# Cross-attention with layer norm on one core: another order of VectorE's work in the prologue

## The chip, the cores and the metric

The kernel runs on one core of one Trainium2 chip. The metric is the device time of one execution in microseconds (us). A core has TensorE (PE; its weight loads are shown apart as PEld), VectorE (DVE), ScalarE (ACT), GpSimd (POOL) and SyncE (SP), whose queue issues most of the DMAs. Each engine works through its own instructions in the order in which the program wrote them, and waits where an input or a buffer is not ready.

## The reference

For a batch of 4 with 2048 queries of width 512 and a context of 77 keys:

```python
qs = (q @ wq).reshape(Bq, Lq, H, HD).transpose(0, 2, 1, 3)
ks_ = (k @ wk).reshape(Bq, Lk, H, HD).transpose(0, 2, 1, 3)
vs = (v @ wv).reshape(Bq, Lk, H, HD).transpose(0, 2, 1, 3)
scores = jnp.einsum('bhqd,bhkd->bhqk', qs, ks_) / jnp.sqrt(jnp.float32(HD))
scores = jnp.where(mask[:, None, :, :], -jnp.inf, scores)
attn_w = jax.nn.softmax(scores, axis=-1)
attn = jnp.einsum('bhqk,bhkd->bhqd', attn_w, vs)
out = attn @ wo + q
mu = jnp.mean(out, axis=-1, keepdims=True)
var = jnp.mean((out - mu) ** 2, axis=-1, keepdims=True)
return (out - mu) / jnp.sqrt(var + EPS) * gamma + beta
```

There are 16 heads of width 32; `q` is x, and `k` and `v` are both the context. All is in float32.

## The kernel before, in words

The 8192 query rows make 64 tiles of 128 rows, 16 tiles to a batch. Two tiles are a pair, four are a group. Products of 512 columns are made in three parts from a high and a low part of each operand (wqh and wql, xth and xtl, and so on). The high part is a copy on ScalarE, the low part a subtraction on VectorE or GpSimd.

The order of the work is written out by hand: the program's order is each engine's order. PSUM is one ring of 8 banks (`bank`), taken in TensorE's order, so a product waits until what lay in its bank eight allocations earlier has been read out. Dependencies go by the region of a tile that an instruction touches.

The **prologue** (lines 558 to 622) loads and splits the inputs and makes the queries of the first group (pq, L591 and `q_visit`, L173) and all keys (pk, `keys_part`, L192), which ScalarE and VectorE copy to kct (`keys_evac`, L205).

The **loop** (lines 635 to 734) takes one pair per pass, u being its first tile. For a tile t the steps are:

- `scores(t)` (L289): 64 matmuls on TensorE into four banks.
- `maxima(t, lo, hi)` (L307): VectorE, 16 instructions (one per head) that add the mask's bias mb and find the row's maximum; they write pbuf, of which there are three.
- `exps(t)` (L324): ScalarE, 16 exponentials with their sums.
- `recip(t)` (L336) on VectorE and `normalise(t)` (L340) on GpSimd.
- `transp(t)` (L359): VectorE, blocks of 32x32 into B. B has two buffers, and the first two uses of them are ctx_f and ctx_h, the context in the prologue.
- `regroup(b)` (L381): twelve DMAs on SP for a pair, from B to PT.
- `av(b)` (L390): the attention product of a pair on TensorE, 32 matmuls from PT and vsb into two banks (pa). `av_hi` and `av_lo` split it for `o_proj` (L452), then come `residual`, `moments`, `scale`, `affine` and `store`, some passes later.

In the first passes other work lies between these steps. `mask_bias(b, ts)` (L277) makes mb from the mask for the tiles ts of a batch, two instructions on VectorE. `mask_nan(b)` (L282) is a row check that makes nz from the mask, three instructions. `split_wv` (L255) makes the low parts of wv on VectorE. `values(r)` (L231) makes the values of batch r on TensorE, 12 matmuls into one bank (pv), and `values_evac(r)` (L240) copies them to vsb with VectorE in two instructions: batch r, and those rows of the last batch that were dealt to the same product. `load_xT`, `cast_xT` and `split_xT` bring a group's x; a new `load_xT` on SP waits until `split_xT` on GpSimd has released its buffer. `split_wo` makes the low parts of wo on GpSimd. `q_visit` and `q_evac` make a quarter of a group's queries: passes 0, 2 and 4 have extra ones (`early`, L625).

From tile 54 on, a written list of steps (`ORDER`, L45) takes the place of the loop. The change does not touch it.

VectorE's order in the first passes is, in the program's order: mask of tile 0, keys, maxima of tile 0 with a q copy in the middle, mask of tiles 1 to 15, low parts of wv, q copy, reciprocal 0, maxima 1, transpose 0, row check, reciprocal 1; then maxima 2 with two q copies in the middle, transpose 1, value copy 0, two q copies, reciprocal 2, maxima 3, value copies 1 and 2, reciprocal 3; then maxima 4, transposes 2 and 3, two q copies, reciprocal 4, maxima 5.

Of the kernel before, what the change touches and what calls it, by code (L numbers as in the profile page):

```python
# [67 lines left out]
def xattn_layernorm(  # L68
# [17 lines left out]
    TPB = mask.shape[2]  # L86
# [57 lines left out]
    def keys_of(h):  # L144
        return slice(TAIL_K, NK2) if h % 2 == 0 else slice(0, NK)
# [3 lines left out]
    od, pos, mvs, rns, vd, ris, ends = {}, {}, {}, {}, {}, {}, {}  # L149


    def load_xT(g, c):
        fx[g, c] = sb.tile([P, 2, GRP], F32, tag="xtf", name=f"xtf_{g}_{c}")
        nc.sync.dma_start(fx[g, c], xT[g, :, c : c + 2])
# [29 lines left out]
    def q_evac(g, m):  # L184
        pq = qp.pop((g, m))
        if g:
            nc.vector.tensor_copy(qd[g][:, m, :], pq)
        else:
            nc.vector.tensor_copy(qd[0][:, m : m + 2, BLK:], pq.rearrange("p (m r) -> p m r", m=2))
# [15 lines left out]
    def keys_evac(pks, m):  # L205
        for i, eng in ((m, nc.scalar), (m + 1, nc.vector)):
            pk = pks[i][:, : NB * (NK + 1)].rearrange("p (b k) -> p b k", b=NB)[:, :, :NK]
            for dst, src in ((kct[:, i, :, TAIL_K:], pk), (kct[:, i, :, :TAIL_K], pk[:, :, NK - TAIL_K :])):
                if eng is nc.scalar:
                    eng.activation(dst, src, AF.Copy, scale=KSCALE)  # L210
                else:
                    eng.tensor_scalar(dst, src, KSCALE, None, ALU.mult)
# [18 lines left out]
    def values(r):  # L231
        pv = bank(f"pv_{r}")
        n = 0
        for c in range(NC_D):
            for i, v in ((0, wvh), (0, wvl), (1, wvh)):
                nc.tensor.matmul(pv, ctx_s[c][i][:, r, :], v[c], start=(n == 0), stop=(n == 11))
                n += 1
        vd[r] = pv

    def values_evac(r):  # L240
        pv = vd.pop(r)
        for b, p0, k0, n in ((r, 0, 0, NK2), (NB - 1, NK2, 32 * r, 32)):
            src, dst = (a.rearrange("p (q a d) -> p q a d", a=2, d=HD) for a in (pv[p0 : p0 + n], vsb[k0 : k0 + n, b]))
            rows_of = vm[k0 : k0 + n, :, 0][:, None, :, None].to_broadcast((n, NP, 2, HD))
            nc.vector.tensor_tensor(dst, src, rows_of, ALU.mult)
# [9 lines left out]
    def split_wv():  # L255
        for c in range(NC_D):
            nc.vector.tensor_tensor(wvl[c], stage_b[:, 0, c], wvh[c].bitcast(F32), ALU.subtract)
# [19 lines left out]
    def mask_bias(b, ts=slice(0, TPB)):  # L277
        mb, nz, m8 = bat[b]
        nc.vector.tensor_scalar(mb[:, ts, TAIL_K:], m8[:, ts], MASKED, None, ALU.mult)
        nc.vector.tensor_scalar(mb[:, ts, :TAIL_K], m8[:, ts, NK - TAIL_K :], MASKED, None, ALU.mult)  # L280

    def mask_nan(b):  # L282
        mb, nz, m8 = bat[b]
        nc.vector.tensor_reduce(nz, m8, AX.X, ALU.min)
        nc.vector.tensor_scalar(nz, nz, 3.0e38, 10.0, ALU.mult, ALU.mult)
        nc.vector.tensor_scalar(nz, nz, 0.0, EPS, ALU.mult, ALU.add)
# [20 lines left out]
    def maxima(t, lo, hi):  # L307
        pb = pbuf[t % NPB]
        mb = bat[t // TPB][0]
        nm = nmax[t]  # L310
        for h in HEADS[lo:hi]:
            g, j = divmod(h, GH)
            nc.vector.tensor_tensor_reduce(  # L313
                pb[:, h // 2, (h % 2) * NK : (h % 2 + 1) * NK],
                scs[t][j][:, g * NK : (g + 1) * NK],
                mb[:, t % TPB, keys_of(h)],
                -1.0,
                3.0e38,
                ALU.add,
                ALU.min,  # L320
                accum_out=nm[:, h : h + 1],
            )
# [13 lines left out]
    def recip(t):  # L336
        ris[t] = sb.tile([P, H], F32, tag="ri", bufs=3, name=f"ri_{t}")
        nc.vector.reciprocal(ris[t], sums[t])  # L338

    def normalise(t):  # L340
        pv = pbuf[t % NPB][:, :, : 2 * NK].rearrange("p q (a k) -> p q a k", a=2)
        rv = ris[t].rearrange("p (q a) -> p q a", a=2)[:, :, :, None]
        nc.gpsimd.tensor_tensor(pv, pv, rv.to_broadcast((P, NP, 2, NK)), ALU.mult)  # L343
# [15 lines left out]
    def transp(t):  # L359
        b, tt = divmod(t, 2)  # L360
        if b not in bts:
            bts[b] = sb.tile([P, 5, 2 * NP * 32], F32, tag="B", name=f"B_{b}")
        if b < NBLK - 1:
            bt = bts[b].rearrange("p c (q t r) -> p c q t r", q=NP, t=2)[:, :, :, tt, :]
        else:
            bt = bts[b].rearrange("p c (t q r) -> p c q t r", q=NP, t=2)[:, :, :, tt, :]
        nc.vector.transpose(  # L367
            bt.rearrange("p c q r -> p q c r"),
            pbuf[t % NPB].rearrange("p q (c r) -> p q c r", c=5),
        )  # L370
# [238 lines left out]
        split(*(a[:, c : c + 2, BLK:] for a in gx[0]), f0[c][:, 1])  # L609
    deal_last()  # L610
    q_visit(0, 0)
    mask_bias(0, slice(0, 1))
    gate(stage_a[:, 1, NC_D - 1, D - 1 :])
    load_wv()
    for m in range(0, NG, 2):
        keys_evac(pks, m)
    for c in range(0, NC_D, 2):
        fx[1, c] = stage_a[:, 0, c : c + 2]
        nc.sync.dma_start(fx[1, c], xT[1, :, c : c + 2])
# [8 lines left out]
    def visits(u):  # L628
        return early[u] if u in early else [divmod(u + 5, 4)] * (u + 5 < 4 * NGRP)

    def pieces(u):
        return casts.get(u) or [((u + 8) // 4, u % 4)] * (u + 8 < 4 * NGRP)

    evac = [(0, 0)]
    for u in range(0, 2 * CUT, 2):
        n = u // 2
        m, k = divmod(u, TPB)

        for q in pieces(u + 2):
            if u >= 4:  # L640
                load_xT(*q)
        for t in (u - 4, u - 3):
            if t >= 0:
                load_x(t)
        scores(u)
        maxima(u, 0, H // 2)
        for q in evac:
            q_evac(*q)
        maxima(u, H // 2, H)
        for q in pieces(u):  # L650
            cast_xT(*q)
        exps(u, 0, H)
        for q in pieces(u):
            split_xT(*q)
        if u == 0:
            mask_bias(0, slice(1, TPB))
            split_wv()
        if u >= 6:
            o_proj(u - 6)
        for v in {2: (0,)}.get(u, ()):  # L660
            values(v)
        for q in visits(u):
            q_visit(*q)
        if u >= 6:
            residual(u - 6)
            moments(u - 6)
        if u == 4:
            transp(2)
        if u == 2:
            load_xT(*pieces(4)[0])  # L670
        if u:
            transp(u - 1)
            regroup(n - 1)
        for v in list(vd):
            values_evac(v)
        if u >= 8:
            scale(u - 8)
            scale(u - 7)
        if u >= 8:
            affine(u - 8)  # L680
        for q in visits(u):
            q_evac(*q)
        if u == 0:
            load_wo()
            nc.gpsimd.memset(ident, 0.0)
            nc.gpsimd.affine_select(ident, ident, [[-1, P]], ALU.not_equal, 1.0, base=0, channel_multiplier=1)
        if k == TPB - 6 and m + 1 < NB:
            load_mask(m + 1)
        if k == TPB - 4 and m + 1 < NB:
            mask_bias(m + 1)  # L690
        if k == TPB - 2 and m + 1 < NB:
            mask_nan(m + 1)

        recip(u)
        if u >= 4:
            av(n - 2)
            av_hi(n - 2, 0)
            av_hi(n - 2, 1)
        scores(u + 1)
        maxima(u + 1, 0, H // 4)  # L700
        if u >= 4:
            av_lo(n - 2, 0)
        maxima(u + 1, H // 4, H // 2)
        if u >= 4:
            av_lo(n - 2, 1)
        maxima(u + 1, H // 2, H)
        normalise(u)
        for c in {0: (0, 1), 2: (2, 3)}.get(u, ()):
            split_wo(c)
        if u >= 8:  # L710
            affine(u - 7)
        exps(u + 1, 0, H // 4)
        exps(u + 1, H // 4, H)
        if u >= 5:
            o_proj(u - 5)
        if u >= 5:
            residual(u - 5)
        if u != 2:
            transp(u)
        for v in {2: (1, 2)}.get(u, ()):  # L720
            values(v)
            values_evac(v)
        evac = visits(u + 1)
        for q in evac:
            q_visit(*q)
        if u >= 5:
            moments(u - 5)
        if u == 0:
            mask_nan(0)
        recip(u + 1)  # L730
        normalise(u + 1)
        if u >= 8:
            store(u - 8)
            store(u - 7)
# [8 lines left out]
    visits = {"Q": q_visit, "q": q_evac}  # L743
# [81 lines left out]
```

## Time and profile before

| what | value |
|---|---|
| time, median of 3 runs | 518.78 us (516.29 to 519.95) |
| the profiled execution's own time | 517.11 us |
| its span in the profile | 515.3 us, mean granted clock 0.996 |
| DMA | 110.24 MB, 214 GB/s |
| TensorE at work from / first scores | 1.18 us / 21.65 us |
| first attention product | 54.58 us |
| last attention product in the loop's form | 474.24 us |

A row of the timeline has the start in us, the duration, engine, line and operation, what it writes and reads by the program's names, and a count where equal neighbours are merged; in brackets stand the idle time just before it and what seems to have ended it. In the page the busy times of each engine, their share of the span and the number of instructions come first, then 40 equal slices of the span with a digit for each (9 is 90% or more). The releaser of a wait is inferred from semaphores; where the named engine had long been done, it was another.

### The profile page before, as it was taken

How to read it: one execution, taken by the hardware profiler on the slowest of the kernel's cores; microseconds unless marked ns; L12 is line 12 of the kernel's file. 1: busy time of each engine (PE TensorE's matmuls, PEld its weight loads, DVE VectorE, ACT ScalarE, POOL GpSimd, SP SyncE). 2: the span in 40 equal slices, each digit the busy share in tenths (PEclk: the TensorE clock that was granted, in tenths of full speed). 3: DMA queues.
4: the chain of work that ended last, by engine and by line, in shares of the span. 5: the costliest groups of instructions: out<-in, count | busy, mean ns of one | idle time of the engine just before them, and what ended most of it. 6: DMA issues, size and time to landing. Idle time of an engine off the chain costs nothing.

```text
span 515.3 us, 20436 instructions
## 1 busy us (share of the span) xinstructions
PE 504.5 (98%) x6838; PEld 385.7 (75%) x6838; DVE 473.8 (92%) x2572; ACT 470.3 (91%) x2241; POOL 418.1 (81%) x375
## 2 busy tenths in 40 slices
PE   9999989999999999999999999999999999999994
PEld 6987767777777777777777777777777877777672
DVE  5699998899999888989999898889999989999996
ACT  6789999999899999999899999999899999999841
POOL 0658549889799988888889989889889988857996
PEclk9999999999999999999999999999999999999998
DMA  8946678787778878788778878869878887776665
GB/s 304 402 146 161 175 201 206 205 233 207 202 186 229 222 217 226 211 215 223 182 208 235 232 199 213 227 178 240 216 201 220 212 217 232 203 200 176 170 215 209
DMA packets 58936, 110.24 MB, mean 214 GB/s; under 512 B 9392, under 2 KB 11312, under 8 KB 58832
## 3 DMA queue, kind: packets, MB, share of 16 engines
q1 hardware_dynamic: 56144, 103.62, 72.6%
q0 software_dynamic: 2128, 4.85, 3.4%
q8 instruction: 55, 0.90, 0.8%
q10 hardware_dynamic: 560, 0.46, 0.3%
q14 instruction: 49, 0.40, 0.3%
HBM read 41.79 MB, written 16.78 MB: 114 GB/s over the span
## 4 chain that ended last, share of the span: by engine, by line
PE 74%; DVE 8%; POOL 5%; DMA 4%; SPq 3%; ACT 3%; issue 2%; DVEq 0%; POOLq 0%; ACTq 0%
PE po L463 30%; PE pq L170 26%; PE pa L397 9%; PE sc L299 9%; ACT pbuf L327 2%; SPq L379 2%; DVE B L367 2%; DMA PT<-B 2%; DVE pbuf L313 2%; DMA stage_b<-wo 1%; DMA stage_a<-wk 1%; POOL mvt L529 1%; POOL o_end L542 1%; DVE AL L432 1%; POOL o_end L493 1%
## 5 line engine op out<-in xcount | busy, mean ns | idle before, releaser
L327 ACT ACTIVATE pbuf<-pbuf,nm 128x77 f32<-128x77 f32 x1024 | 352.4, 349 | 17.3 <-DVE nm L313 15.8
L327 ACT ACTIVATION_READ_ACCUMULATOR pbuf<-pbuf,nm 128x1 f32 x1024 | 194.0, 189 | 0.0
L313 DVE CUSTOM_DVE_ANT_0 pbuf<-sc,mb 128x77 f32<-128x77 f32 x1024 | 170.5, 230 | 22.3 <-PE sc L299 22.2
L343 POOL TENSOR_TENSOR pbuf<-pbuf,ri 128x1232 f32<-128x1232 f32 x63 | 142.2, 2258 | 23.5 <-DVE ri L338 19.4
L170 PE MATMUL pq<-xth,wqh 128*128 128x512 f32 (+1 forms) x256 | 98.8, 386 | 0.0
L170 PE MATMUL pq<-xtl,wqh 128*128 128x512 f32 (+1 forms) x256 | 97.9, 382 | 0.0
L170 PE MATMUL pq<-xth,wql 128*128 128x512 f32 (+1 forms) x256 | 97.9, 382 | 0.0
L367 DVE STREAM_TRANSPOSE B<-pbuf 128x1280 f32<-128x1280 f32 x64 | 95.5, 1493 | 2.2 <-DMA PT<-B 1.7
L463 PE MATMUL po<-woh,AH 128*128 128x512 f32 x232 | 96.8, 417 | 0.0
L463 PE MATMUL po<-wol,AH 128*128 128x512 f32 x232 | 90.7, 391 | 0.0
L463 PE MATMUL po<-woh,AL 128*128 128x512 f32 x232 | 88.8, 391 | 0.0
L313 DVE DVE_READ_ACCUMULATOR2_ANT nm<- 128x1 f32 x1024 | 83.9, 82 | 0.0
L493 POOL TENSOR_TENSOR o<-o,gam 128x512 f32<-128x512 f32 x50 | 65.6, 1312 | 14.4 <-ACT o L489 14.3
L299 PEld LDWEIGHTS sc<-kct,q 32*64 32x64 f32 x4096 | 51.4, 130 | 24.2 <-issue 23.5
L494 POOL TENSOR_TENSOR o<-o,bet 128x512 f32<-128x512 f32 x50 | 64.5, 1289 | 3.9
L163 POOL TENSOR_TENSOR xtl<-xtf,xth 128x1024 fp32r<-128x1024 f32 x28 | 67.0, 2394 | 0.0
L299 PE MATMUL sc<-kct,q 32*64 32x77 f32 x4096 | 61.5, 237 | 0.3 <-DVE nm L313 0.3
L397 PE MATMUL pa<-PT,vsb 96*32 96x256 f32 x960 | 58.0, 382 | 1.9 <-DVE st L471 1.3
L170 PEld LDWEIGHTS pq<-xth,wqh 128*128 128x128 f32 x256 | 48.1, 188 | 9.8
L170 PEld LDWEIGHTS pq<-xth,wql 128*128 128x128 f32 x256 | 48.1, 188 | 9.4
L170 PEld LDWEIGHTS pq<-xtl,wqh 128*128 128x128 f32 x256 | 48.1, 188 | 9.1
L463 PEld LDWEIGHTS po<-woh,AH 128*128 128x128 f32 x232 | 43.5, 187 | 12.5 <-issue 0.7
(139 smaller groups left out, 700.5 us busy)
## 6 DMA issues: line engine op xcount, KB each, us to landing
PT<-B SPq DMA_DIRECT2D x352, 128.0 KB
xtf<-xT SPq DMA_DIRECT2D x28, 512.0 KB
o<-x SPq DMA_DIRECT2D x56, 256.0 KB
out<-o SPq DMA_DIRECT2D x56, 256.0 KB
PT<-B POOLq DMA_DIRECT2D x20, 128.0 KB, 4.0
o_end<-x SPq DMA_DIRECT2D x8, 256.0 KB
out<-o_end SPq DMA_DIRECT2D x8, 256.0 KB
xtf<-xT SPq DMA_DIRECT2D x4, 256.0 KB
```

The source lines that it names most:

```text
L163: nc.gpsimd.tensor_tensor(l, fx.pop((g, c)), h.bitcast(F32), ALU.subtract)
L170: nc.tensor.matmul(pq, w[:, c, m * P : (m + 1) * P], r[:, c, rs], start=(n == 0), stop=(n == 11))
L299: nc.tensor.matmul(sc[j][half : half + P // 2, g * NK : (g + 1) * NK], qs[q, g, r0 : r0 + P // 2], kct[q, g, t // TPB, keys_of(j)], start= ...
L313: nc.vector.tensor_tensor_reduce(pb[:, h // 2, (h % 2) * NK : (h % 2 + 1) * NK], scs[t][j][:, g * NK : (g + 1) * NK], mb[:, t % TPB, keys_ ...
L327: nc.scalar.activation(pb[:, h // 2, (h % 2) * NK : (h % 2 + 1) * NK], pb[:, h // 2, (h % 2) * NK : (h % 2 + 1) * NK], AF.Exp, bias=nmax[t ...
L343: nc.gpsimd.tensor_tensor(pv, pv, rv.to_broadcast((P, NP, 2, NK)), ALU.mult)
L367: nc.vector.transpose(bt.rearrange("p c q r -> p q c r"), pbuf[t % NPB].rearrange("p q (c r) -> p q c r", c=5),)
L379: queue.dma_start(pts[b][32 * c : 32 * c + 32, i, :, cols], src)
L397: nc.tensor.matmul(pas[b, g // 2][HD * j : HD * (j + 1), (g % 2) * BLK : (g % 2 + 1) * BLK], vsb[:, 2 * b // TPB, HD * h : HD * (h + 1)], ...
L463: nc.tensor.matmul(pos[t], a[:, c, rs], w[:, c, :], start=(first and n == 0), stop=(n == 11))
L493: nc.gpsimd.tensor_tensor(o, o, gam, ALU.mult)
L494: nc.gpsimd.tensor_tensor(o, o, bet, ALU.add)
```

## The change

Seven edits, all in VectorE's order of the first three passes, with the GpSimd and DMA steps that go along:

- The first piece of the mask covers tiles 0 to 7 (before: tile 0); the rest, tiles 8 to 15, stays in pass 0.
- The row check of batch 0 stands behind the key copies in the prologue (before: behind transpose 0).
- The low parts of wv and reciprocal 0 stand behind the second tile's maxima (before: ahead of them).
- Reciprocal 1 and normalise 1 stand between the halves of the third tile's maxima (before: at the end of pass 0).
- Transpose 0 moves to the second pass, then value copy 0, then transpose 1; the two q copies of that pass move behind the maxima of tile 3.
- Value copy 1 follows its product; transpose 2 stands at the end of the second pass, ahead of the maxima of tile 4 (before: behind them).
- Value copy 2 moves behind transpose 3 and the second regroup.

```diff
-    mask_bias(0, slice(0, 1))
+    mask_bias(0, slice(0, TPB // 2))
...
         keys_evac(pks, m)
+    mask_nan(0)
...
         maxima(u, 0, H // 2)
+        if u == 2:
+            recip(1)
+            normalise(1)
         for q in evac:
             q_evac(*q)
...
         if u == 0:
-            mask_bias(0, slice(1, TPB))
-            split_wv()
+            mask_bias(0, slice(TPB // 2, TPB))
...
-        if u == 4:
-            transp(2)
         if u == 2:
             load_xT(*pieces(4)[0])
+        if u == 2:
+            transp(0)
+            values_evac(0)
         if u:
             transp(u - 1)
             regroup(n - 1)
-        for v in list(vd):
-            values_evac(v)
+        if u == 4:
+            values_evac(2)
...
-        for q in visits(u):
-            q_evac(*q)
+        if u != 2:
+            for q in visits(u):
+                q_evac(*q)
...
-        recip(u)
+        if u:
+            recip(u)
...
         maxima(u + 1, H // 2, H)
+        if u == 0:
+            split_wv()
+            recip(0)
+        if u == 2:
+            for q in visits(u):
+                q_evac(*q)
         normalise(u)
...
-        if u != 2:
+        if u >= 4:
             transp(u)
-        for v in {2: (1, 2)}.get(u, ()):
-            values(v)
-            values_evac(v)
+        if u == 2:
+            values(1)
+            values_evac(1)
+            values(2)
...
-        if u == 0:
-            mask_nan(0)
-        recip(u + 1)
-        normalise(u + 1)
+        if u:
+            recip(u + 1)
+            normalise(u + 1)
+        if u == 2:
+            transp(2)
```

## The prediction

> **What bounds the kernel now.** I read the page first (busy shares and slices), then what TensorE waits for, then the timelines of all engines up to 100 us, and the chain of waits last. TensorE is busy for almost the whole span, and the granted clock is full in nearly every slice:
>
> ```profile
> PE 504.5 (98%) x6838; PEld 385.7 (75%) x6838; DVE 473.8 (92%) x2572; ACT 470.3 (91%) x2241; POOL 418.1 (81%) x375
> PEclk9999999999999999999999999999999999999998
> ```
>
> The ends of matmuls are modelled, so a busy share alone proves little. The next rows do more. First the busy times of each engine in stretches (PE, PEld, DVE, ACT, POOL, then clock, DMA share, GB/s), then TensorE's instructions in order of time, then its two waits of over 0.3 us in the whole run, of which the second is before its first instruction:
>
> ```profile
> 67.00:67.50 0.50, 0.00 (x0) 0.00 (x0) 0.47 (x2) 0.50 (x4) 0.50 (x1) 1.00 0.58 209
> 83.20:98.20 15.00, 15.00 (x211) 11.39 (x210) 13.43 (x79) 14.51 (x71) 13.21 (x12) 1.00 0.81 221
> ```
>
> ```profile
> 54.58 1.93 PE L397 MATMUL pa<-PT,vsb 96*32 96x256 f32 x32
> ...
> 66.30 0.39 PE L170 MATMUL pq<-xtl,wqh 128*128 128x512 f32 x1
> 66.53 0.39 PE L170 MATMUL pq<-xth,wql 128*128 128x512 f32 x1
> 68.22 0.42 PE L397 MATMUL pa<-PT,vsb 96*32 96x256 f32 x4 [1.30 <-DVE st L471]
> ...
> 83.20 1.93 PE L397 MATMUL pa<-PT,vsb 96*32 96x256 f32 x32
> ```
>
> ```profile
> PE pa L397 <- DVE st L471: 1.3, 1, 1.3
> PE pw L565 <- DVE ident L558: 1.2, 1, 1.2
> ```
>
> Equal matmuls start 0.23 us apart though each lasts 0.39 (66.30, 66.53): they follow at TensorE's own pace. From one attention product to the next (68.22, 83.20, end of the stretch at 98.20) a pair of tiles takes 15.0 us, all of it TensorE, while ScalarE has 14.51 of work in the stretch and VectorE 13.43. So in the steady loop TensorE sets the time. An earlier VectorE gains nothing there. In the prologue, too, TensorE runs without a wait from about 5 us to 66.92 (66.53 + 0.39). Then it stands still for 1.30 us, ahead of the second pair's attention product. **That one gap is all that a new order of VectorE's prologue can win.** The row names bn_stats (DVE st), but the product does not read it; it reads PT, which the SP queue's transfers write:
>
> ```profile
> 41.19 0.33 SPq L154 DMA_DIRECT2D xtf<-xT  x1
> 41.62 8.86 SPq L379 DMA_DIRECT2D PT<-B  x12
> ...
> 51.15 0.92 SPq L446 DMA_DIRECT2D o<-x  x2
> 56.17 9.22 SPq L379 DMA_DIRECT2D PT<-B  x12
> 65.48 0.53 SPq L154 DMA_DIRECT2D xtf<-xT  x1
> ```
>
> ```profile
> 49.88 2.69 DMA PT<-B
> ```
>
> The first regroup starts at 41.62 and by the chain of waits (second fence) lands at 52.57, 10.95 us later; its product runs at 54.58. The second starts at 56.17, as soon as the transposes below end at 56.13; the product starts at 68.22, 12.05 us later. I take 10.95 to 12.05 us from start of a regroup to data.
>
> **The change, part by part.** VectorE's rows that carry the sums:
>
> ```profile
> 16.79 0.19 DVE L279 TENSOR_SCALAR mb<-m 128x77 bf16<-128x77 uint8 x1
> ...
> 18.01 0.62 DVE L212 TENSOR_SCALAR kct<-pk 128x308 f32<-128x308 f32 x2 [0.95 <-PE pk L196]
> 18.89 0.62 DVE L212 TENSOR_SCALAR kct<-pk 128x308 f32<-128x308 f32 x2 [0.26 <-PE pk L196]
> 22.59 0.24 DVE L313 CUSTOM_DVE_ANT_0 pbuf<-sc,mb 128x77 f32<-128x77 f32 x1 [3.07 <-PE sc L299]
> ...
> 25.72 1.35 DVE L279 TENSOR_SCALAR mb<-m 128x1155 bf16<-128x1155 uint8 x1
> ...
> 27.21 1.28 DVE L257 TENSOR_TENSOR wvlAH<-stage_b,wvh 128x512 fp32r<-128x512 f32 x2
> ...
> 29.61 0.68 DVE L189 COPY q<-pq 128x512 f32<-128x512 f32 x1
> 30.21 0.24 DVE L338 RECIPROCAL ri<-sum 128x16 f32<-128x16 f32 x1
> 32.85 1.50 DVE L367 STREAM_TRANSPOSE B<-pbuf 128x1280 f32<-128x1280 f32 x1
> 34.28 1.39 DVE L284 TENSOR_REDUCE nz<-m 128x16 f32<-128x1232 uint8 x1
> ...
> 36.21 0.25 DVE L338 RECIPROCAL ri<-sum 128x16 f32<-128x16 f32 x1
> ...
> 42.87 1.29 DVE L187 COPY q<-pq 128x512 f32<-128x512 f32 x2
> ...
> 46.71 2.81 DVE L245 TENSOR_TENSOR vsb<-pv,small 96x512 f32<-96x512 f32 x4
> ...
> 53.23 2.90 DVE L367 STREAM_TRANSPOSE B<-pbuf 128x1280 f32<-128x1280 f32 x2 [0.19 <-issue]
> ```
>
> Unit costs from these starts: both mask instructions for 15 tiles 1.49 (25.72 to 27.21); the row check 1.93 (34.28 to 36.21); low parts of wv 2.40 (27.21 to 29.61); 16 maxima with a reciprocal 2.64 (30.21 to 32.85); a transpose 1.43; two q copies 1.25; one value evacuation (two of the four instructions) 1.4. Nothing is added or removed but the split of the mask (still two pairs of instructions); no DMA is added. The other engines:
>
> ```profile
> 30.59 0.36 ACT L327 ACTIVATE pbuf<-pbuf,nm 128x77 f32<-128x77 f32 x1 [2.11 <-DVE nm L313]
> 36.08 1.99 ACT L159 CAST xth<-xtf 128x1024 fp32r<-128x1024 f32 x2
> ```
>
> ```profile
> 30.54 2.26 POOL L343 TENSOR_TENSOR pbuf<-pbuf,ri 128x1232 f32<-128x1232 f32 x1 [4.41 <-DVE ri L338]
> 32.76 2.55 POOL L267 TENSOR_TENSOR wol<-stage_b,woh 128x512 fp32r<-128x512 f32 x2
> 36.54 2.26 POOL L343 TENSOR_TENSOR pbuf<-pbuf,ri 128x1232 f32<-128x1232 f32 x1 [1.24 <-DVE ri L338]
> 38.77 4.74 POOL L163 TENSOR_TENSOR xtl<-xtf,xth 128x1024 fp32r<-128x1024 f32 x2
> ```
>
> ```profile
> 32.16 0.95 PE L299 MATMUL sc<-kct,q 32*64 32x77 f32 x64
> 41.44 0.95 PE L299 MATMUL sc<-kct,q 32*64 32x77 f32 x64
> 48.01 0.95 PE L299 MATMUL sc<-kct,q 32*64 32x77 f32 x64
> ```
>
> *Mask and row check.* Eight tiles' mask from 16.79 cost about 0.8 (half of 1.49), at most all of it: done by 17.6, latest 18.3, against the key copies at 18.01, which wait for TensorE. A slip of 0.3 is covered: the first maxima stand idle for 3.07 us until 22.59. The row check from 19.5 (18.89 + 0.62) ends at 21.4, also ahead of 22.59. Price zero.
>
> *Second tile's maxima ahead of the low parts.* From 25.72: mask half 0.8, q copy 0.6, so the maxima run from 27.2 to 29.7 instead of 30.4 to 32.85. ScalarE is free at 28.5 (30.59 less its idle 2.11), and starts the second tile's exponentials 2.1 earlier; they take 5.5 (30.59 to 36.08): 28.5 to 34.0. The low parts run 29.7 to 32.1, the reciprocal to 32.3. Who waits for the low parts: TensorE's first value product, just behind the scores at 32.16, thus 33.1. Slack 1 us.
>
> *GpSimd and SP.* The first normalise starts at 32.3 instead of 30.54; two normalises, two wo parts and the first xT half keep GpSimd busy until 41.8 instead of 41.2. The xT load on SP (41.19) waits for that half, and the regroup stands behind it: 42.2 instead of 41.62. It lands at 53.2 (10.95 later) to 54.3, and TensorE wants it at 54.58. Hidden, with 0.3 to 1.4 to spare.
>
> *The next pair on VectorE.* Scores at 32.16 end at 33.1. First half of the maxima to 34.4, reciprocal 1, two q copies, second half: 37.1. Transpose 0 to 38.5, value evacuation 0 to 39.9, transpose 1 to 41.4 (normalise 1 ends 39.4). Exponentials of tile 2, behind ScalarE's casts, 36.0 to 41.5. Maxima of tile 3 when the scores at 41.44 end: 42.4 to 44.9 (before: from 44.2). The two q copies moved behind them end at 46.2, and TensorE wants them for the scores at 48.01: slack 1.8. Value evacuation 1 to 47.6. Exponentials of tile 3 end at 48.1, reciprocal 3 to 48.4. Transpose 2 overwrites the buffer of ctx_h, which the last value product reads until 48.0: 48.4 to 49.9. Maxima of tile 4 to 52.4, transpose 3 to 53.9, against 56.13 before.
>
> *What this is worth.* The second regroup starts at 53.9, 2.2 earlier; SP is free by 52.7 (its loads end at 52.07, plus 0.6). Data is there at 64.9 to 66.0; TensorE arrives at 66.92. The gap of 1.30 closes with about 1 us to spare.
>
> *What is late next.* Value evacuation 2 now stands behind transpose 3: 53.9 to 55.3. It frees the bank of the second half of the first attention product, which starts about 0.96 after 54.58, at 55.5. Cost 0, with only 0.2 to spare; from below it cannot gain, from above I allow 0.5. The third regroup (started at 69.70, so data 80.7 to 81.8) now meets TensorE at 81.9 instead of 83.20: 0 to 0.2 lost at worst.
>
> **Sum.** 1.30 less 0 (at worst 0.7) leaves 1.3 us. The profiled execution took 517.11 us (span 515.3 and 1.8 around it): 515.8. The median shown is 518.78 of 516.29 to 519.95, 1.67 above it; taking off the same 1.3 gives 517.5, the number I predict.
>
> The Trainium skill, "Perfetto Trace Analysis", section "Identifying the Most-Contended Engine", speaks against my bound: it says that matmul busy share is a poor measure of headroom and weight-load share a good one. By that the 75% of PEld would leave room in TensorE, and the time would be that of the third rival below. The 15.00 us loop without a gap speaks against it.
>
> **Rivals.**
> Given back or not closed in full: the third regroup, or the tail, which the chain of waits puts on GpSimd, keeps part of it. 0.3 to 1.0 us less: about 518.1.
> The wait at 66.92 is not the transfer's: then nothing changes, 518.8. For it: the row names VectorE. Against: the named instruction isn't read there.
> TensorE has hidden slack, and VectorE's whole lead of 2.2 to 2.3 counts: 516.5. Against: the 0.23 pace.
> Slower: value evacuation 2 behind transpose 3 holds TensorE inside the first attention product. It decides from an evacuation that ends 1.3 past 55.5, thus at 56.8, if VectorE runs 1.5 later than my replay. At 2.5 late, TensorE loses 2.3 there, the old gap is covered, net +1.0: 519.8.
>
> One more slower case needs a stall far longer: TensorE standing for some microseconds and then running on at a lower clock. The row at 67.00 shows the clock at 1.00 within the gap of 1.30, so a stop of that size costs only itself. The Trainium skill, "TensorE: Matmul & The Clock Gate", section "HAM oscillation — how this bites in real kernels", says that gaps above roughly 3.4 us throttle the clock; no run here shows one. With 3.4 lost and as much again at half pace it would be an estimated 5.1, less the 1.3: about 522.6.
>
> **How the numbers follow.** Gap closes: 0.62 (517.5). In part: 0.17 (518.1). No effect: 0.08 (518.8). Hidden slack: 0.04 (516.5). Slower at the evacuation: 0.07 (519.8). A stall not foreseen that costs over 1%: 0.02. About 1%, 5 us, is what a measurement of this kernel can tell from no change; only the last reaches it. The runs spread by 2.5 below and 1.2 above their median, so 517.5 gives 515.0 to 518.7; the partial, neutral and part of the slower case take the upper end to 519.5. Slower by over 1%: 0.04, with a share for what a replay cannot see; faster by over 1%: 0.02, since the gap is all there is to win; within: 0.94.
>
> **What would show it.** First maxima still at 22.59; tile 1's exponentials from 28.5; low parts behind the second tile's maxima with TensorE's value product still at 33.0; the second regroup on SP at about 54; the second attention product at 66.9 with no idle time, the third at 81.9. I am wrong if TensorE shows a wait between 22 and 66 us (look at 33, 48 and 55.5 first), if the 1.3 stays with an earlier regroup, or if it comes back at 81.9.

## The result and the profile after

The changed kernel takes 524.76 us in the median of 4 runs (523.88 to 526.04), the one before 518.68 (4 runs): 1.0134 of the time, 95% interval 1.0103 to 1.0165. It was forecast 1.3 us faster, at 517.5; it is 6.1 us slower, outside the range. The profiled execution, the slowest of the four, took 526.04 us (span 524.2).

What TensorE waited for, in total, by the profile of the changed kernel (us, times, longest):

```profile
PE sc L299 <- DVE vsb L245: 2.1, 1, 2.1
PE sc L299 <- DVE nm L313: 1.3, 4, 0.4
PE pa L397 <- DVE nm L313: 1.2, 1, 1.2
PE pw L565 <- DVE ident L558: 1.2, 1, 1.2
PE po L463 <- issue: 0.9, 1, 0.9
PE pa L397 <- PE pq L170: 0.6, 1, 0.6
```

The old wait ahead of the second attention product is gone. In its place stand waits at scores and ahead of and inside the first product. All but two are put down to VectorE: the 0.9 at a projection (issue), and the 0.65 ahead of the first product, which comes as the first regroup's data land. TensorE's rows in order of time show where (the second and third products end the list):

```profile
33.64 0.95 PE L299 MATMUL sc<-kct,q 32*64 32x77 f32 x64
...
56.78 1.07 PE L397 MATMUL pa<-PT,vsb 96*32 96x256 f32 x16 [0.65 <-PE pq L170]
59.06 1.07 PE L397 MATMUL pa<-PT,vsb 96*32 96x256 f32 x16 [1.21 <-DVE nm L313]
60.06 0.58 PE L299 MATMUL sc<-kct,q 32*64 32x77 f32 x4
60.96 0.48 PE L299 MATMUL sc<-kct,q 32*64 32x77 f32 x2 [0.32 <-DVE nm L313]
63.58 1.37 PE L299 MATMUL sc<-kct,q 32*64 32x77 f32 x58 [2.13 <-DVE vsb L245]
...
66.33 0.63 PE L170 MATMUL pq<-xth,wqh 128*128 128x512 f32 x1
66.75 0.63 PE L170 MATMUL pq<-xtl,wqh 128*128 128x512 f32 x1
...
75.68 1.93 PE L397 MATMUL pa<-PT,vsb 96*32 96x256 f32 x32
...
90.68 1.93 PE L397 MATMUL pa<-PT,vsb 96*32 96x256 f32 x32
```

Set against the rows of before, TensorE is 1.5 us late at the third scores (33.64 against 32.16), 2.2 at the first product (56.78 against 54.58) and 7.5 at the second (75.68 against 68.22), with the closed gap of about 1.3 already taken off. The third is at 90.68 against 83.20, again 7.5: the loss is all made by 69 us, and the loop then runs at the same 15 us a pair. The rest, up to the 8.9 between the two profiled executions (526.04 and 517.11), comes far later, with the 0.9 at a projection (issue) that this execution has and the one before has not.

The matmuls at 66.33 and 66.75 start 0.42 apart, where they stood 0.23 apart before. The clock (the column behind POOL's) says why:

```profile
59.00:60.20 1.20, 1.14 (x18) 0.64 (x18) 1.20 (x17) 1.20 (x8) 0.00 (x0) 1.00 0.02 7
60.20:61.50 1.30, 0.93 (x6) 0.52 (x5) 1.30 (x9) 1.30 (x9) 0.00 (x0) 0.74 0.00 0
61.50:63.50 2.00, 0.00 (x0) 0.00 (x0) 1.99 (x3) 2.00 (x13) 0.00 (x0) 0.50 0.04 8
...
66.00:67.00 1.00, 1.00 (x4) 0.81 (x3) 1.00 (x10) 1.00 (x8) 1.00 (x1) 0.50 0.89 205
67.00:68.00 1.00, 1.00 (x4) 0.76 (x4) 1.00 (x8) 1.00 (x8) 0.52 (x1) 0.67 0.92 209
68.00:69.00 1.00, 1.00 (x6) 0.62 (x4) 1.00 (x11) 1.00 (x7) 0.00 (x0) 1.00 0.83 197
```

A mean of 0.74 over 60.20 to 61.50 and of 0.67 over 67.00 to 68.00 puts the clock at 0.50 from about 60.8 to 67.7. So TensorE lost twice: standing, and running at half the clock. The second loss is about 2 us by my estimate (half of the 4.1 us from 63.58 to 67.7). The clock fell before the longest stop began: the 2.13 us run from 61.45 to 63.58. Now VectorE, where it starts, and GpSimd beside it:

```profile
16.91 0.47 DVE L279 TENSOR_SCALAR mb<-m 128x616 bf16<-128x616 uint8 x1
...
19.57 1.42 DVE L284 TENSOR_REDUCE nz<-m 128x16 f32<-128x1232 uint8 x1
21.03 2.37 DVE L285 TENSOR_SCALAR nz<-nz 128x16 f32<-128x16 f32 x1
23.43 2.32 DVE L286 TENSOR_SCALAR nz<-nz 128x16 f32<-128x16 f32 x1
25.67 0.23 DVE L313 CUSTOM_DVE_ANT_0 pbuf<-sc,mb 128x77 f32<-128x77 f32 x1
...
34.88 0.23 DVE L338 RECIPROCAL ri<-sum 128x16 f32<-128x16 f32 x1
...
56.66 1.51 DVE L367 STREAM_TRANSPOSE B<-pbuf 128x1280 f32<-128x1280 f32 x1 [5.71 <-DMA PT<-B]
...
62.17 1.36 DVE L245 TENSOR_TENSOR vsb<-pv,small 96x512 f32<-96x512 f32 x2
```

```profile
20.99 4.73 POOL L163 TENSOR_TENSOR xtl<-stage_a,xth 128x1024 fp32r<-128x1024 f32 x2 [5.62 <-ACT xth L159]
```

SP's queue, and the end of the first regroup in the chain of waits:

```profile
44.55 0.33 SPq L154 DMA_DIRECT2D xtf<-xT  x1
44.98 8.19 SPq L379 DMA_DIRECT2D PT<-B  x12
...
62.27 7.86 SPq L379 DMA_DIRECT2D PT<-B  x12
```

```profile
52.58 3.90 DMA PT<-B
```

Two things are new. The row check's two steps on 16 elements take 2.37 and 2.32 us, not 0.17, and the first maxima start at 25.67, not 22.59. And transpose 2 stands 5.71 us for a DMA from B (the first regroup, which ends at 52.58 + 3.90 = 56.48), ahead of all that VectorE still had to do for tiles 4 and 5. The second regroup starts at 62.27, 6.1 later than before, not 2.2 earlier.

The two causes that I then tested: **A**, the row check's steps wait for GpSimd's subtractions, because both engines need a port in common. L285 ends at 23.40, halfway through GpSimd's two instructions, which end at 25.72; L286 ends at 25.75. **B**, the second pair's B lies in the same buffer as the first pair's, so transpose 2 has to wait until the first regroup has read it. The compiled program names the waits of the transposes 0 to 3 on VectorE:

```
L367 StreamTranspose B_0_687<-pbuf0_77 128x8x5x32 [waits Pool_49]
L367 StreamTranspose B_0_687<-pbuf1_78 128x8x5x32 [waits Pool_49]
L367 StreamTranspose B_1_813<-pbuf2_79 128x8x5x32 [waits DMAHW4_49,DMAHW3_49,DMAHW5_49,DMAHW2_49,DMAHW6_49,DMAHW1_49,DMAHW7_49,DMAHW0_49,Pool_49]
L367 StreamTranspose B_1_813<-pbuf0_77 128x8x5x32 [waits Pool_49]
```

Its placement gives B_0 and B_1 the same address (109568), with ctx_f there before them, and ctx_h and later B_2 the other (119808). It does so in both kernels.

### The profile page after: what moved, and what is told of

Read it like the earlier page. It is cut to its first block, busy times and chain, and to the rows that moved or that the text cites. A ratio compares the mean times of both kernels' runs of the same rounds, so it can differ in the third digit from the quotient of the medians.

```text
span 524.2 us, 20430 instructions
## 1 busy us (share of the span) xinstructions
PE 508.8 (97%) x6838; PEld 388.0 (74%) x6838; DVE 477.7 (91%) x2572; ACT 470.2 (90%) x2241; POOL 418.0 (80%) x375
## 4 chain that ended last, share of the span: by engine, by line
PE 80%; DVE 6%; POOL 4%; ACT 4%; SPq 2%; DMA 2%; issue 1%; DVEq 0%; POOLq 0%
PE po L463 31%; PE pq L170 27%; PE sc L299 10%; PE pa L397 9%; ACT pbuf L327 3%; SPq L379 2%; DMA PT<-B 2%; DVE B L367 2%; PE pk L196 1%; DVE pbuf L313 1%; PE pq L591 1%; POOL mvt L529 1%; PE pw L565 1%; POOL o_end L542 1%; POOL o_end L493 0%
## 5 line engine op out<-in xcount | busy, mean ns | idle before, releaser
L327 ACT ACTIVATION_READ_ACCUMULATOR pbuf<-pbuf,nm 128x1 f32 x1024 | 197.3, 193 | 0.0
L299 PEld LDWEIGHTS sc<-kct,q 32*64 32x64 f32 x4096 | 52.9, 131 | 28.0 <-issue 24.5
L299 PE MATMUL sc<-kct,q 32*64 32x77 f32 x4096 | 63.8, 239 | 3.4 <-DVE vsb L245 2.1
```

Source lines behind the costliest of these rows:

```text
L299: nc.tensor.matmul(sc[j][half : half + P // 2, g * NK : (g + 1) * NK], qs[q, g, r0 : r0 + P // 2], kct[q, g, t // TPB, keys_of(j)], start= ...
L327: nc.scalar.activation(pb[:, h // 2, (h % 2) * NK : (h % 2 + 1) * NK], pb[:, h // 2, (h % 2) * NK : (h % 2 + 1) * NK], AF.Exp, bias=nmax[t ...
```

## Experiments

Times are medians. Ratios are against runs of the kernel before on the same chip, whose medians were 518.68 for the changed kernel, 517.18 for the next four rows of the table, 517.41 for the four after them and 517.17 for the last two. The starts of the attention products in the profiled execution tell more than the times, since from the third one to the end of the span every run takes 431.5 to 433.5 us, but for "before, transpose 2 early" with 438.1. The executions don't start alike, though: TensorE's first scores start between 21.65 and 22.46. So the last column counts the third product from the first scores, and gives the difference to before. Two profiles of the kernel before differ by 0.3 in it.

| run | time, us | ratio, 95% interval | first scores | second product | third product | third from first scores, against before |
|---|---|---|---|---|---|---|
| before | 518.68 |  | 21.65 | 68.22 | 83.20 |  |
| after | 524.76 | 1.0134 (1.0103 to 1.0165) | 21.79 | 75.68 | 90.68 | +7.3 |
| row check ahead of the keys | 522.68 | 1.0123 (1.0090 to 1.0156) | 22.02 | 72.57 | 87.56 | +4.0 |
| own buffers | 517.46 | 1.0017 (1.0000 to 1.0033) | 22.05 | 69.99 | 85.03 | +1.4 |
| both | 517.09 | 1.0010 (0.9982 to 1.0038) | 22.46 | 67.66 | 82.67 | -1.3 |
| row check at the pass's end | 522.71 | 1.0138 (1.0072 to 1.0204) | 21.88 | 73.13 | 88.12 | +4.7 |
| before, row check moved | 518.84 | 1.0032 (1.0011 to 1.0053) | 21.72 | 69.48 | 84.47 | +1.2 |
| before, transpose 2 early | 520.10 | 1.0069 (1.0032 to 1.0106) | 21.75 | 69.54 | 84.76 | +1.5 |
| before, own buffers | 517.12 | 0.9996 (0.9977 to 1.0015) | 21.73 | 67.17 | 82.18 | -1.1 |
| transpose 2 back | 521.82 | 1.0082 (1.0053 to 1.0110) | 22.45 | 72.37 | 87.36 | +3.4 |
| value copy 2 ahead | 521.75 | 1.0078 (1.0056 to 1.0099) | 21.77 | 74.39 | 89.36 | +6.0 |
| before again (one profile) | 517.30 |  | 21.86 | 68.69 | 83.70 | +0.3 |

**Row check ahead of the keys** (in the changed kernel):

```diff
+    mask_nan(0)
     for m in range(0, NG, 2):
         keys_evac(pks, m)
-    mask_nan(0)
```

> The changed kernel with the row check moved from behind the key copies to ahead of them (VectorE free there from 17.5 us; GpSimd idle until 21; DMA at about 400 GB/s). Theory A (the two 16-element steps of the row check stood 2.37 and 2.32 us because GpSimd's subtraction L163 held a port that both share): both steps take 0.17, first maxima at 22.7 instead of 25.7, no wait of TensorE at the second scores. Rival A' (they were slow from the DMA traffic): still above 2 us each, keys and first scores late. Theory B (transpose 2 waits for the first regroup, because both pairs' B lie in one buffer) leaves a wait of about 5 us there. Time by A and B: 522 to 523; by A': 525 or more.

VectorE in this run, the small steps first:

```profile
19.14 0.17 DVE L285 TENSOR_SCALAR nz<-nz 128x16 f32<-128x16 f32 x1
19.35 0.17 DVE L286 TENSOR_SCALAR nz<-nz 128x16 f32<-128x16 f32 x1
22.96 0.24 DVE L313 CUSTOM_DVE_ANT_0 pbuf<-sc,mb 128x77 f32<-128x77 f32 x1 [2.38 <-PE sc L299]
...
53.96 1.51 DVE L367 STREAM_TRANSPOSE B<-pbuf 128x1280 f32<-128x1280 f32 x1 [4.97 <-DMA PT<-B]
```

With GpSimd idle (its subtraction starts at 20.39) and the DMA engines busy (375 GB/s from 19 to 20 us) the steps are back at 0.17, as A has it. The third product is 3.1 earlier than in the changed kernel. The wait of transpose 2 stays, 4.97, and TensorE then waits 2.30 at the scores of tile 5, until 60.88; the clock is at 0.50 again from about 60.6 to 64.

**Own buffers.** The context's high part moves into four buffers of the tag o that are free then; B keeps its two buffers for itself and ctx_f.

```diff
-    ctx_h = sb.tile([P, NC_D, NB, P], F32R, tag="B", name="ctx_h")
+    ctx_h = [sb.tile([P, NB, P], F32R, tag="o", bufs=8, name=f"ctx_h{c}") for c in range(NC_D)]
...
-    ctx_s = [[ctx_h[:, c], ctx_2[c // 2][:, c % 2]] for c in range(NC_D)]
+    ctx_s = [[ctx_h[c], ctx_2[c // 2][:, c % 2]] for c in range(NC_D)]
...
-        for a in (ctx_h, *ctx_2):
+        for a in (*(h[:, None] for h in ctx_h), *ctx_2):
```

> The changed kernel with the context's high part moved out of B's two buffers (into four free o buffers), so that the second pair's B no longer lies where the first pair's lies. Same order of all steps; three more small copies on ScalarE near 16 us. Theory B: transpose 2 starts at about 51 instead of 56.7, no wait of TensorE at the scores of tile 5, clock stays at 1.00; the row check's 4.5 us stay. TensorE loses 1.5 at the second scores and 0.7 at the first attention product and wins the old gap of 1.3: 519.6. Rival B' (transpose 2 waits for something else, such as the value products or GpSimd): the wait stays near 5 us, time 524 to 525.

VectorE's reciprocal 3 and transposes 2 and 3 in this run:

```profile
50.13 0.25 DVE L338 RECIPROCAL ri<-sum 128x16 f32<-128x16 f32 x1 [0.85 <-ACT pbuf L327]
50.30 1.45 DVE L367 STREAM_TRANSPOSE B<-pbuf 128x1280 f32<-128x1280 f32 x1
54.33 1.50 DVE L367 STREAM_TRANSPOSE B<-pbuf 128x1280 f32<-128x1280 f32 x1
```

Transpose 2 follows its reciprocal without a wait, and TensorE's wait at the scores of tile 5 is gone: B is shown. The clock stays at 1.00. The time falls to 517.46, though the long row check is still there (1.56 and 2.32). The third product is still 1.8 later than before, 1.4 if counted from the first scores; 1.16 of that is one wait (issue) of TensorE near 63, which no theory here explains.

**Both edits.**

> Both edits: row check ahead of the keys and own buffers. If A and B are the whole cause, the run is what was predicted: no wait of TensorE between 22 and 66 us, second regroup near 54, second attention product without a gap near 66.9, 517.4 against 518.7 before. If a third cause is there (value copy 2 behind transpose 3, reciprocals late), a wait of TensorE remains between 48 and 60 and the time is 519 or more.

```profile
49.34 1.45 DVE L367 STREAM_TRANSPOSE B<-pbuf 128x1280 f32<-128x1280 f32 x1
53.37 1.51 DVE L367 STREAM_TRANSPOSE B<-pbuf 128x1280 f32<-128x1280 f32 x1
```

```profile
54.90 9.32 SPq L379 DMA_DIRECT2D PT<-B  x12
```

```profile
55.39 1.93 PE L397 MATMUL pa<-PT,vsb 96*32 96x256 f32 x32
...
67.66 1.93 PE L397 MATMUL pa<-PT,vsb 96*32 96x256 f32 x32
```

This is the run that the prediction described, 0.8 us late from the first scores on. Transpose 3 starts at 53.37, the second regroup at 54.90, and the second product follows without a wait, 12.27 behind the first (before: 13.64). With A and B removed nothing of the loss is left at the products, so they are its cause. Counted from the first scores, the third product is 1.3 earlier than before, as forecast. Two things are not shown by this run. The time shows no gain: 1.3 us would be a ratio of 0.9975, just outside the interval. And the new order need not be what closes the gap: the control below keeps the old order, has the same buffers, and is 1.1 earlier.

**Row check at the end of pass 0** (the changed kernel, `mask_nan(0)` under `if u == 0` at the end of the pass, where it stood before; reciprocal 1 now comes later).

> The changed kernel with the row check at the end of pass 0, behind reciprocal 0: GpSimd is then at normalise 0 and the wo parts without a pause, and the DMA engines are idle. Theory A: the two small steps again end only when GpSimd's instructions end, 1 to 2.3 us each; first maxima at 22.7. Rival A' (DMA traffic): 0.17 each. Time by A: the third tile's maxima start near 36 instead of 35, wait at transpose 2 stays, 522 to 526; by A': 521 to 523.

VectorE, then GpSimd:

```profile
33.71 1.04 DVE L285 TENSOR_SCALAR nz<-nz 128x16 f32<-128x16 f32 x1
34.78 1.22 DVE L286 TENSOR_SCALAR nz<-nz 128x16 f32<-128x16 f32 x1
```

```profile
32.46 2.25 POOL L343 TENSOR_TENSOR pbuf<-pbuf,ri 128x1232 f32<-128x1232 f32 x1 [5.88 <-DVE ri L338]
34.68 2.54 POOL L267 TENSOR_TENSOR wol<-stage_b,woh 128x512 fp32r<-128x512 f32 x2
```

L285 ends at 34.75, normalise 0 at 34.71; L286 ends at 36.00, after the first half of the two wo parts. Now GpSimd is busy and the DMA engines are nearly idle, and the steps are long again. DMA traffic is ruled out; A is shown from both sides, as far as it says that the steps wait for GpSimd's instruction; that a port is the reason no trace shows. Not every VectorE instruction waits: the reduction of the row check (L284) took 1.37 beside normalise 0 here, about what it takes elsewhere (1.39 before). The time, 522.71, lies in both forecasts and decides nothing. The same place was harmless in the kernel before because GpSimd had a pause from 35.3 to 36.5, where the steps happened to fall:

```profile
35.70 0.17 DVE L285 TENSOR_SCALAR nz<-nz 128x16 f32<-128x16 f32 x1
35.91 0.17 DVE L286 TENSOR_SCALAR nz<-nz 128x16 f32<-128x16 f32 x1
```

**The kernel before with one part alone.** First the row check behind the key copies, then transpose 2 ahead of the maxima of tile 4:

```diff
         keys_evac(pks, m)
+    mask_nan(0)
...
-        if u == 0:
-            mask_nan(0)
```

> The kernel before with one part of the change alone: the row check behind the key copies. Theory A (the shared port): its two small steps again end with GpSimd's two subtractions, first maxima at 25.7 instead of 22.6, the second tile's maxima at 33.5 instead of 30.4, TensorE waits 2 to 3 at the third scores. Third attention product 2 to 4 later than before (83.20), time 2 to 4 more. Rival (the step was hidden, as the prediction had it): within 0.5.

```diff
-        if u == 4:
-            transp(2)
...
         normalise(u + 1)
+        if u == 2:
+            transp(2)
```

> The kernel before with transpose 2 alone moved ahead of the maxima of tile 4. Theory B: it waits for the first regroup to land (52.6), about 2.3 behind the reciprocal at 50.3; maxima 4 end at 56.7, transpose 3 at 58.2 instead of 56.1; the gap ahead of the second product grows from 1.3 to about 3. Third product 2 to 3 later, time 2 to 3 more. Rival (only the long row check makes the early transpose harmful): within 0.5.

The row check alone costs 1.3 at the third product (ratio 1.0032), less than the 2 to 4 that I expected. Transpose 2 alone waits 2.71 and costs 1.6 there, less than the expected 2 to 3. In the time it costs more, 2.7 by the median and 3.6 by the ratio of 1.0069: three of the ten executions took 524.7 to 526.7. The profiled one is among them; TensorE stands in it for 3.6 (issue) at projections, far behind the third product, and why is open. Both together with the rest of the change cost 7.5: the late reciprocal 0 delays GpSimd, GpSimd the xT load on SP, the load the first regroup (44.98 against 41.62), and transpose 2 waits for the end of that regroup. About 2 of the 7.5 is the halved clock, which neither part alone brought on. So together they cost more than the sum of the two.

**The control: before with own buffers.**

> The kernel before with the buffers of the earlier run of that name: a control for the three more copies on ScalarE. Theory: third product within 0.5 of 83.20, the gap of 1.3 ahead of the second product stays, time within 0.5 of before. If it is faster by 1 or more, the second run's gain was not the wait of transpose 2.

The second regroup on SP and the second product, first in the control, then in a second profile of the kernel before (its expectation stands below):

```profile
55.97 8.98 SPq L379 DMA_DIRECT2D PT<-B  x12
67.17 1.93 PE L397 MATMUL pa<-PT,vsb 96*32 96x256 f32 x32 [0.24 <-PE pq L170]
```

```profile
56.42 9.31 SPq L379 DMA_DIRECT2D PT<-B  x12
68.69 1.93 PE L397 MATMUL pa<-PT,vsb 96*32 96x256 f32 x32 [1.62 <-DVE mv L476]
```

**Transpose 2 back** behind the maxima of tile 4, in the changed kernel:

> The changed kernel with transpose 2 back behind the maxima of tile 4; the long row check and the one buffer stay. Theory B: it still waits for the first regroup (56.5), so maxima 4 run at 51 and do not wait, but transpose 3 and value copy 2 end near 61, and TensorE's scores of tile 5 wait about 2 for that copy's bank. Third product near 88 (after: 90.7), time 521 to 523. Rival (the place ahead of the maxima is the whole cost): 85, time 519.

The control's time is that of before. The gap ahead of the second product did not stay, though: 0.2. With transpose 2 back the changed kernel still loses 4.2 at the third product, 3.4 if counted from the first scores. TensorE waits 1.9 for value copy 2, so the place ahead of the maxima is not the whole cost; as long as the first regroup lands at 56, VectorE is late in either order.

**Value copy 2 ahead of reciprocal 3** in the changed kernel, and the kernel before again:

```diff
-        if u == 4:
-            values_evac(2)
...
             values(2)
+            values_evac(2)
```

> The changed kernel with value copy 2 ahead of reciprocal 3 and transpose 2, where VectorE waits for ScalarE anyway. The long row check and the one buffer stay, so transpose 2 still waits until about 56.6 and the maxima of tile 4 still end near 60.8. Theory (VectorE's late maxima are the path, the bank of value copy 2 is only the place where TensorE feels it): the 2.1 wait at the scores of tile 5 goes, TensorE waits soon after instead (scores of tile 6 or the first projection), third product 88 to 90 (after: 90.7), time 522 to 524. Rival (the bank of value copy 2 is a loss of its own): third product 87 or earlier, time 521 or less.

> The kernel before, unchanged, for a second profile. In the control with own buffers the gap ahead of the second product shrank from 1.30 to 0.2 though the second regroup started only 0.2 earlier. Theory: the gap depends on how long the regroup's twelve issues and the last landing take in one execution, so it comes out between 0.2 and 1.5 here, and what was to be won was not a fixed 1.3. Rival: it is 1.2 to 1.4 again, and own buffers are worth 1 us by themselves.

The wait for value copy 2 goes and others come: 1.3 in four pieces at the scores of tile 5, 1.0 at a query product for its bank, the clock down again (0.64 between 60 and 65). The third product is at 89.36, 1.3 better. In the time more is won, about 2.9 us by the two ratios (1.0134 and 1.0078), and 521.75 lies between the two forecasts. So most of the loss is VectorE's lateness, and the bank mainly the place where it was felt.

In the second profile of the kernel before the gap is 1.62, above what either side expected. Two profiles of it gave 1.30 and 1.62, the control 0.2 with a regroup that started only 0.2 to 0.5 earlier: from start of the second regroup to the product it took 12.05, 12.27 and 11.20. Why own buffers would shorten that is open; the times, 0.9996 (0.9977 to 1.0015), do not decide whether the 1 us at the products is worth anything. No version here beats the kernel before by more than its measurement can tell.

## Why the prediction was wrong, step by step

- *TensorE sets the time in the loop, and the prologue can win only the one gap.* Right for the loop: from the second product to the third every version takes 15.0 to 15.2 us. With the causes removed the gap closed, but nearly so in the control with the old order too; beyond the control the new order is 0.2 earlier at the third product, less than two profiles of one kernel differ, and no time shows a gain. The bound holds only for what can be won; the loss had no such bound.
- *Mask and row check, "Price zero".* This step failed first: a cost put at nothing. The row check's 1.93 came from a place where GpSimd stood idle (35.3 to 36.5); at its new place GpSimd was at the subtractions of group 1, and it took 6.2 (19.57 to 25.75). I used the duration of a row without the neighbours that made it. The Trainium skill, "SBUF — State Buffer", section "Who interferes with whom", has the rule: VectorE's tensor_scalar can take the port pair that it has in common with GpSimd, and whichever starts second waits until the other's whole instruction is over. The trace of the changed kernel agrees in that the second step ends 0.03 us behind GpSimd's second instruction (25.75 and 25.72), and the first step at 23.40, just after that second instruction starts (23.33). The mask halves went better than priced: 0.47 and 0.23.
- *"Transpose 2 overwrites the buffer of ctx_h".* This step failed with the larger cost: with this cause removed the third product came 5.9 earlier, with the row check's removed 3.3, both counted from the first scores. Transpose 2 overwrites the buffer of the first pair and waited until 56.5 for its regroup, not until 48.0 for the value products. I counted buffers in the program's order of use; the placement had chosen otherwise. The row that I quoted for the landing, 49.88 2.69 DMA PT<-B, held the clue: the chain goes on from it at 52.57 into VectorE, and transpose 2 follows at 53.23 after a wait of 0.19. In the kernel before this wait was covered by the maxima of tile 4; the change took away the cover.
- *GpSimd and SP, first regroup at 42.2.* The mechanism held, the size did not: the late row check and reciprocal made it 44.98, and with A removed 42.40.
- *Value evacuation 2 behind transpose 3.* The slower rival named the right instruction. It was felt at the scores of tile 5 (2.13), not inside the product, and it came late because transpose 2, ahead of the maxima or behind them, waited for the first regroup. I gave VectorE 1.5 to 2.5 of lateness; value copy 2 started at 62.17 instead of 53.9, 8.3 late.
- *The clock.* The prediction held that a stop of 1.3 costs only itself, which the old and the repeated profile bear out (1.30 and 1.62). It saw no cost in several shorter stops. In the changed kernel the clock fell to 0.50 at about 60.8, behind stops of 0.65 and 1.21 and within one of 0.32, all begun after 56.1, and ahead of the stop of 2.13. The 3.4 us gap that the Trainium skill gives ("TensorE: Matmul & The Clock Gate", section "HAM oscillation — how this bites in real kernels") was not reached by any of them: here shorter ones, close together, were enough.
- *The chances.* A replay by hand of one engine's order had 0.2 to 1 us of slack at four places, and each place rested on a row taken from other neighbours. A chance of 0.04 for slower by over 1% was far too small for that.

## What to carry to other kernels

Before an instruction is moved, look at what the other engines do at the new place, not only at whether its own engine is idle there: a 16-element step of 0.17 us can stand for 2.3 us behind GpSimd. When a writer is moved ahead, find out from the compiled program which buffer it writes and who read it last, and look in the trace for waits that are now covered by just the work that moves behind it. And when several moves shift one chain, price them together: here 1.3 and 1.6 apart became 7.5 in the whole change.

## What the runs showed of the hardware

- A short VectorE instruction held up by GpSimd ends with GpSimd's instruction: 1.04, 1.22, 1.55, 2.32 and 2.37 us for work of 0.17 us. The row shows the wait as the instruction's own duration, not as idle time.
- The granted clock fell to 0.50 in five runs. The longest stops of TensorE near it were 2.13 us in the changed kernel, 2.30 in both with the row check at another place, 1.90 with transpose 2 back, and 1.02 with value copy 2 ahead. Worked out from means over stretches, it stayed at 0.50 for 3.4 us in three of them and for 6.8 in two (the changed kernel and value copy 2 ahead). It fell 0.6 us before the longest stop began in the changed kernel, and 1.7 us after it had ended with transpose 2 back (at 62.2, the stop until 60.43). Stops of 1.30 and 1.62 alone left it at 1.00. What sets the moment was not tested.
- The mask instruction for 8 tiles took 0.47 us for 616 elements, that for 15 tiles 1.35 for 1155: 1.31 against 0.86 elements per ns. Whether the even number of tiles is the reason is not shown; no run varied it by itself.
